# Attention scores of the second and third layer turned by the DMA crossbar instead of TensorE

## The chip, the core and the metric

The kernel runs on one core of a Trainium2 chip. A core has five engines with queues of their own: TensorE (PE in the profile; its weight loads are PEld), VectorE (DVE), ScalarE (ACT), GpSimd (POOL) and SyncE (SP), which here only issues DMA transfers. Each engine works through its queue in order and waits on semaphores for the others. The metric is the device time of one execution in microseconds; the lower, the better. A kernel's time is the median of several executions, and one more execution was taken with the profiler.

## What is computed

Input are 128 graphs of 128 nodes with 256 features each, and their adjacency matrices. Four layers follow one another; each adds its result to its input and normalizes. The first is a gated graph network of three steps, the other three are graph attention:

```python
# layer 0: three times
m = jnp.einsum('bnd,de->bne', h, weight[i])
aggr = jnp.einsum('bst,bsd->btd', A, m)
h = _gru_cell(aggr, h, w_ih, w_hh, b_ih, b_hh)
...
# layers 1 to 3
Wh = jnp.einsum('bnf,of->bno', h, W)
e = f_i[:, :, None] + f_j[:, None, :]
e = jnp.where(e > 0, e, ALPHA * e)
e = jnp.where(adj == 0, NEG_INF, e)
attention = jax.nn.softmax(e, axis=2)
h_prime = jnp.einsum('bij,bjo->bio', attention, Wh)
...
x = _layernorm(x + layer(x, adj), axis=-1)
```

Everything is float32.

## The kernel before

Four graphs make a group (G = 4), so there are 32 groups (NG). A tile of one group has 128 partitions and mostly 4x128 or 4x256 columns.

For a group, `gru` runs three steps (STEPS). A step aggregates with the adjacency matrix (L566), then makes the gates by a Strassen scheme of seven products (L508, function `strassen`): its products go to PSUM tiles of the kind "gate", which ScalarE (L574, L578, L581, L592, L605) and VectorE (L513, L615) read. Several products are added into one gate tile, so that the next product into a tile has to wait until the last value was read: `kept` copies the first product out by L574 (whole) or by L578 and L581 (in halves). Elementwise work on VectorE and GpSimd follows (L608 to L631).

Then `gat` runs three attention layers (l = 0, 1, 2). The vectors f come from VectorE (L677), are multiplied by the factor `rstd` of the layer before (L681, l > 0), turned (L689) and spread over partitions by GpSimd (L696). VectorE adds the mask (L712), ScalarE makes leaky ReLU (L716) and the exponentials with their sums (L733) into the tile `e_`. The scores must then be transposed to `pT`, because TensorE needs them with the other index on partitions (L774 multiplies by them, L785 by the layer's weights; L791 adds the residual). The normalization of a layer isn't carried out in full: its factor `rstd`, one value for each node, is multiplied onto the scores when they are transposed (l > 0). `power` computes it on GpSimd (L425).

There are two ways to transpose. Through TensorE: four transposes into a PSUM tile of the kind "bank" (L744), and an eviction which for l > 0 multiplies by `rstd` on the way (`scaled`, L749 on VectorE or four L753 on ScalarE). Through the DMA crossbar (`turned`): a copy that puts the two 16-bit halves of each number apart (L402), one crossbar transfer (L403), and a copy that puts them together again (L406). The copies appear as L299, L301 and L397 with 1024 elements of uint16. Before the change the crossbar served the turned input of groups, the GRU's state between steps, and the scores of layer l = 0; the last four groups (LAST = 4) use TensorE throughout.

The order of all instructions is made before the kernel runs, by a planner (class `Plan`). Each operation is entered with the engines it may run on and an assumed duration for each, with the tiles that it reads and writes, and with a due time. `order` plays the whole list through: an engine that is idle takes the ready operation with the earliest due time, if its buffers are free. So an engine's queue, the choice between engines, and the buffers' numbers follow from these settings:

- `LATER` gives each of a group's six stages (three GRU steps, three attention layers) a due time relative to the group's number. In the last four groups the stages go in lockstep.
- `MARGIN` is extra time in ns, after which TensorE takes an operation to be ready. `LATENCY` is that of hand-overs.
- `pools` says how many buffers of each kind there are ("gate" and "bank" share the eight PSUM banks), and `own` how many of them the oldest stage keeps for itself.
- `port`: VectorE and GpSimd share a way to memory. An operation on an engine named in its `port` starts in the plan only when no other such operation holds it. By default only GpSimd is named; most large VectorE operations on SBUF name both.

Of the kernel before, what the change touches and what calls it, by code (L numbers as in the profile page):

```python
# [13 lines left out]
ALU = mybir.AluOpType  # L14
AX = mybir.AxisListType

P = 128
D = 256
KC = D // P
G = 4  # L20
GN = G * P
H = GN // 2
STEPS = 3
# [26 lines left out]
class Plan:  # L50
# [5 lines left out]
    LATENCY = {"PE": 250, "ACT": 220, "DVE": 200, "POOL": 250, "SP": 4000}  # L56

    RUSH = 0.5
    MARGIN = 300

    def __init__(self, slots, own):
        self.free = {t: list(range(n)) for t, n in slots.items()}
# [3 lines left out]
        self.readers = {}  # L66

    def op(self, engines, fn, reads=(), writes=(), prio=0, lag=0, port=("POOL",), start=0, room=()):

        rush = self.RUSH if any((k[0] if isinstance(k, tuple) else k).tag in ("gate", "bank") for k in reads) else 0  # L70
        o = Op(engines, fn, (prio[0] - rush, len(self.ops)), lag, port)
        o.group = prio[1]
        o.earliest = start
        norm = lambda k: k if isinstance(k, tuple) else (k, 0)
        for k in map(norm, reads):
            if k in self.writer:
                o.deps.add(self.writer[k])
            self.readers.setdefault(k, []).append(o)
            o.bufs.append(k[0])
        for k in map(norm, writes):  # L80
            if k in self.writer:
                o.deps.add(self.writer[k])
            o.deps.update(self.readers.pop(k, ()))
            self.writer[k] = o
            o.bufs.append(k[0])
        o.bufs.extend(room)
        o.deps.discard(o)
        o.bufs = [b for b in dict.fromkeys(o.bufs) if b.tag]
        for b in o.bufs:
            b.left += 1  # L90
        self.ops.append(o)
# [113 lines left out]
def adj_resnorm_kernel(  # L205
# [14 lines left out]
    nc = tc.nc  # L220
    B = x.shape[0]
    NG = B // G
    LAST = 4
# [3 lines left out]
    psum = ctx.enter_context(tc.tile_pool(name="psum", bufs=1, space=bass.MemoryType.PSUM))  # L227


    pools = {"gru": 4, "xs": 2, "am": 5, "k2": 28, "k4": 18, "f": 4, "mv": 4, "st": 6, "v": 24,  # L230
             "gate": 5, "bank": 3}
    own = ({"k2": 7, "k4": 8, "gate": 1, "bank": 1, "v": 5, "st": 0}, {"k2": 5, "k4": 2, "bank": 1, "v": 5, "st": 0})
    floats = {"gru": 0, "k4": 1024, "xs": 1024, "f": 128, "mv": 8, "st": 6, "v": 4}
    tags = {t: (n, floats.get(t, 512)) for t, n in pools.items()}
    U16 = mybir.dt.uint16
    BOTH = ("DVE", "POOL")
    LATER = (-0.25, 1, -0.5, -0.5, 0, 0.25)
    plan = Plan({t: n for t, (n, _) in tags.items()}, own)
    slots = {t: [(psum if t in ("gate", "bank") else work).tile([P, w], F32, name=f"{t}{i}")
                 for i in range(n)] for t, (n, w) in tags.items() if w}  # L240
# [1 line left out]
    def T(b):  # L242
        if b.at is None:
            width = 1
            for s in b.shape:
                width *= s
            at = slots[b.tag][b.slot][:, 0:width]
            if len(b.shape) == 2:
                at = at.rearrange("p (a b) -> p a b", b=b.shape[-1])
            elif len(b.shape) == 3:  # L250
                at = at.rearrange("p (a b c) -> p a b c", b=b.shape[-2], c=b.shape[-1])
            b.at = at
        return b.at
# [133 lines left out]
    def turned(src, keys, dst, prio):  # L387


        rows = Buf("k2", GN)  # L390
        flat = lambda: T(dst) if len(dst.shape) == 1 else T(dst).rearrange("p b q -> p (b q)")
        halves_of = lambda at: at.bitcast(U16).rearrange("p (h b q) -> p h b q", h=2, b=G)
        pairs_of = lambda at: at.bitcast(U16).rearrange("p b (q h) -> p h b q", h=2)

        def together(e):
            if e == "ACT":
                nc.scalar.copy(flat().bitcast(U16).rearrange("p (q h) -> p q h", h=2),  # L397
                               T(rows).bitcast(U16).rearrange("p (h q) -> p q h", h=2))
            else:
                copy(e, flat().bitcast(U16).rearrange("p (q h) -> p h q", h=2),  # L400
                     T(rows).bitcast(U16).rearrange("p (h q) -> p h q", h=2))
        plan.op(APART, lambda e: copy(e, halves_of(flat()), pairs_of(src())), reads=keys, writes=[dst], prio=prio, port=BOTH)  # L402
        plan.op({"SP": 1200}, lambda e: nc.sync.dma_start_transpose(  # L403
            T(rows).bitcast(U16).rearrange("p (a q) -> p a q", q=P), flat().bitcast(U16)),
            reads=[dst], writes=[rows], prio=prio, lag=TURN)
        plan.op(TOGETHER, together, reads=[rows], writes=[dst], prio=prio, port=BOTH)  # L406
# [259 lines left out]
    def gat(g, xc, no, stage):  # L666


        ve, rstd = None, None
        for l in range(3):  # L670
            prio = stage(g, STEPS + l)
            if g == 0:
                score_weights(l, (prio[0], -2))
            f = Buf("f", G, P // G)
            for h in (1, 0):
# [4 lines left out]
                if l:  # L680
                    plan.op({"DVE": 100}, lambda e, h=h, f=f, rstd=rstd: nc.vector.tensor_mul(  # L681
                        T(f)[:, :, 1 - h], T(f)[:, :, 1 - h], T(rstd)), reads=[(f, 2 * b + h) for b in range(G)] + [rstd],
                        writes=[(f, 2 * b + h) for b in range(G)], prio=prio)
            e_, pT, y = Buf("k2", G, P), Buf("k2", G, P), Buf("k4", G, D)
            top, nmax, den, rden = Buf("v", G), Buf("v", G), Buf("v", G), Buf("v", G)
            b_ = bank()
            if g < NG - LAST:

                plan.op({"PE": 115}, lambda e, b_=b_, f=f: nc.tensor.transpose(  # L689
                    T(b_)[:, 0:P], T(f).rearrange("p b h -> p (b h)"), ident),  # L690
                    reads=[(f, 2 * b + 1) for b in range(G)], writes=[b_], prio=prio)
                row = Buf("k2", P)
                plan.op({"ACT": 250, "DVE": 200}, lambda e, b_=b_, row=row: copy(e, T(row), T(b_)[:, 0:P]),
                        reads=[b_], writes=[row], prio=prio)
                for b in range(G):
                    plan.op({"POOL": 300}, lambda e, row=row, b=b, e_=e_: nc.gpsimd.partition_broadcast(  # L696
                        T(e_)[:, b, :], T(row)[b * P // G:b * P // G + 1, 0:P]), reads=[row], writes=[(e_, b)], prio=prio)
                if g == NG - LAST - 1 and l == 2:

                    plan.op({"POOL": 7000}, lambda e: nc.gpsimd.load_library(library_config.standard),  # L700
                            reads=[(e_, b) for b in range(G)], writes=[Buf(None)], prio=prio)
                rows, keys, port = (lambda b, e_=e_: T(e_)[:, b, :]), lambda b: [], BOTH
            else:
                def fn(e, b_=b_, f=f):
                    for b in range(G):
                        nc.tensor.transpose(T(b_)[:, b * P:(b + 1) * P],
                                            T(f)[:, b, 0:1].to_broadcast([P, P]), ident)
                plan.op({"PE": 440}, fn, reads=[(f, 2 * b + 1) for b in range(G)], writes=[b_], prio=prio)
                rows, keys, port = (lambda b, b_=b_: T(b_)[:, b * P:(b + 1) * P]), lambda b, b_=b_: [b_], ("POOL",)
# [5 lines left out]
            for b in range(G):  # L715
                plan.op({"ACT": 285}, lambda e, b=b, f=f, e_=e_: nc.scalar.activation(  # L716
                    T(e_)[:, b, :], T(e_)[:, b, :], AF.Prelu, bias=T(f)[:, b, 1:2], alpha=SLOPE),
                    reads=[(f, 2 * b), (e_, b)], writes=[(e_, b)], prio=prio)
            if l == 1:
# [4 lines left out]
                    reads=[(top, b) for b in range(G)], writes=[some], prio=prio)  # L724
            plan.op({"DVE": 100}, lambda e, f=f, top=top: nc.vector.scalar_tensor_tensor(
                T(top), T(top), -1.0, T(f)[:, :, 1], op0=ALU.mult, op1=ALU.subtract),
                reads=[(top, b) for b in range(G)] + [(f, 2 * b) for b in range(G)],
                writes=[(top, b) for b in range(G)], prio=prio)
            plan.op({"DVE": 100}, lambda e, top=top, nmax=nmax: nc.vector.scalar_tensor_tensor(  # L729
                T(nmax), T(top), SLOPE, T(top), op0=ALU.mult, op1=ALU.min),  # L730
                reads=[(top, b) for b in range(G)], writes=[nmax], prio=prio)
            for b in range(G):
                plan.op({"ACT": 390}, lambda e, b=b, e_=e_, nmax=nmax, den=den: nc.scalar.activation(  # L733
                    T(e_)[:, b, :], T(e_)[:, b, :], AF.Exp, bias=T(nmax)[:, b:b + 1],
                    accum_out=T(den)[:, b:b + 1]), reads=[(e_, b), nmax], writes=[(e_, b), (den, b)], prio=prio)
            by_xbar = g < NG - LAST and l == 0
            if by_xbar:
                turned(lambda e_=e_: T(e_), [(e_, b) for b in range(G)], pT, prio)
            else:
                b_ = bank()  # L740

                def fn(e, b_=b_, e_=e_):
                    for b in range(G):
                        nc.tensor.transpose(T(b_)[:, b * P:(b + 1) * P], T(e_)[:, b, :], ident)  # L744
                plan.op({"PE": 440}, fn, reads=[(e_, b) for b in range(G)], writes=[b_], prio=prio)
                if l:
                    def scaled(e, b_=b_, pT=pT, rstd=rstd):
                        if e == "DVE":
                            nc.vector.tensor_mul(T(pT), T(b_).rearrange("p (b j) -> p b j", b=G),  # L749
                                                 T(rstd).unsqueeze(2).to_broadcast([P, G, P]))  # L750
                        else:
                            for b in range(G):
                                nc.scalar.mul(T(pT)[:, b, :], T(b_)[:, b * P:(b + 1) * P], T(rstd)[:, b:b + 1])  # L753
                    plan.op({"DVE": 630, "ACT": 1100}, scaled, reads=[b_, rstd], writes=[pT], prio=prio)
                else:
                    plan.op(EVICT, lambda e, b_=b_, pT=pT: copy(e, T(pT).rearrange("p b j -> p (b j)"), T(b_)),
                            reads=[b_], writes=[pT], prio=prio)
# [38 lines left out]
            rstd = power(ve, prio)  # L796
# [6 lines left out]
    def stage(g, n):  # L803

        tail = NG - LAST
        return g + LATER[n] if g < tail else tail + n, 2 * g + (n >= STEPS)

    for g in range(NG):
        gat(g, *gru(g, stage), stage)
# [50 lines left out]
```

## Time and profile before

| what | value |
|---|---|
| median of 3 executions | 2603.02 us (2602.8 to 2604.25) |
| the profiled execution | 2601.8 us, span 2600.0 us |
| granted TensorE clock | 0.998 |
| DMA moved | 117.79 MB, mean 45 GB/s |
| crossbar transfers (L403) | 200, median 3.1 us from issue to landing |
| transposes of scores on TensorE (L744) | 272 |
| their eviction with the factor | 228 L753 on ScalarE, 0.380 us each; 7 L749 on VectorE, 0.688 us each |

The span goes from the first instruction to the last. In the listings that follow, a line of a group gives the source line, the engine, the operation, written tile <- read tiles, and shapes; "x4" is the number of instructions. A line in order of time begins with its start and its duration in us, and has in brackets how long its engine was idle before it, and what ended that wait. A float32 matmul stands as two records. The durations of neighbours on one engine overlap a little, since an instruction's end is noted after the next may have begun.

### The profile page before, as it was taken

The page shows a single profiled execution, that of the slowest core. Times are in us where ns is not written, and L with a number is a line of the kernel's source. Part 1 is how long each engine was busy: PE and PEld are TensorE (multiplying, and loading weights), DVE is VectorE, ACT ScalarE, POOL GpSimd, SP SyncE. Part 2 cuts the span into 40 slices and gives each one's busy share as a digit, 9 for nine tenths or more (in the row PEclk, how much of TensorE's full clock was granted, in tenths as well). Part 3 has the DMA queues.
Part 4 walks back from the last instruction along what each step waited for, and adds up shares of the span by engine and source line. Part 5 has one row for each costly group of instructions (what it writes and reads, how often), then busy time and mean ns, then how long its engine had stood idle before and what let it go on. Part 6 is the DMA issues. An engine that isn't in the chain of part 4 may idle for free.

```text
span 2600.0 us, 41538 instructions
## 1 busy us (share of the span) xinstructions
PE 2549.3 (98%) x13484; PEld 2257.3 (87%) x13484; DVE 2124.2 (82%) x6262; ACT 1856.4 (71%) x4750; POOL 601.7 (23%) x866
## 2 busy tenths in 40 slices
PE   8999999999999999999999999999999999999988
PEld 7888888888888888888888888888888888888877
DVE  6688888978888888888888888888888887867687
ACT  5667776877778677777777776777786776665467
POOL 2022222322222221222212222212222211322011
PEclk9999999999999999999999999999999999999999
DMA  5211121312122211222121222121222121100001
GB/s 138 61 38 45 38 48 40 72 41 46 41 49 58 48 39 46 49 50 53 41 49 42 53 49 53 42 45 42 49 58 49 37 49 42 21 13 25 17 1 34
DMA packets 281307, 117.79 MB, mean 45 GB/s; under 512 B 213888, under 2 KB 279424, under 8 KB 281088
## 3 DMA queue, kind: packets, MB, share of 16 engines
q1 hardware_dynamic: 280656, 115.12, 19.1%
q8 instruction: 106, 1.74, 0.3%
q14 instruction: 113, 0.93, 0.1%
q10 hardware_dynamic: 432, 0.01, 0.0%
HBM read 45.89 MB, written 16.78 MB: 24 GB/s over the span
## 4 chain that ended last, share of the span: by engine, by line
PE 82%; DVE 10%; ACT 4%; issue 2%; DMA 1%; POOL 0%; POOLq 0%; ACTq 0%; SPq 0%; DVEq 0%
PE gate L508 59%; PE bank L785 11%; PE bank L774 6%; PE bank L566 4%; DVE k L712 2%; ACT k L733 2%; DVE nobody L677 1%; PE bank L650 1%; DVE k L513 1%; DVE k L301 1%; DVE k L791 1%; PE bank L744 1%; ACT k L299 1%; DVE v L729 1%; DVE v L722 1%
## 5 line engine op out<-in xcount | busy, mean ns | idle before, releaser
L508 PE MATMUL gate<-k,whs 128*128 128x256 f32 x4032 | 1203.3, 380 | 18.1 <-ACT k L574 15.8
L508 PE MATMUL gate<-k,wcs 128*128 128x256 f32 x4032 | 1199.3, 379 | 0.0
L508 PEld LDWEIGHTS gate<-k,wcs 128*128 128x128 f32 x4032 | 766.0, 190 | 104.2 <-issue 0.2
L508 PEld LDWEIGHTS gate<-k,whs 128*128 128x128 f32 x4032 | 736.5, 190 | 115.5 <-ACT k L574 22.5
L513 DVE TENSOR_TENSOR k<-gate,k 128x512 f32<-128x512 f32 x576 | 390.3, 684 | 145.3 <-PE gate L508 124.0
L785 PE MATMUL bank<-gwT,k 128*128 128x256 f32 x1536 | 348.7, 380 | 1.3 <-DVE k L301 1.2
L785 PEld LDWEIGHTS bank<-gwT,k 128*128 128x128 f32 x1536 | 290.5, 190 | 42.4 <-DVE k L301 2.9
L677 DVE SCALAR_TENSOR_TENSOR nobody<-k,wa 128x256 f32<-128x256 f32 x768 | 293.7, 428 | 23.1 <-ACT k L444 21.7
L425 POOL TENSOR_TENSOR v<-v,neghalf 128x4 f32<-128x4 f32 x128 | 136.0, 1062 | 731.8 <-DVE v L463 375.7
L452 ACT ACTIVATE nobody<-k 128x256 f32<-128x256 f32 x384 | 156.2, 408 | 193.2 <-DVE k L791 192.3
L299 ACT COPY k<-bank 128x512 f32<-128x512 f32 (+1 forms) x314 | 177.0, 566 | 136.9 <-PE bank L566 79.2
L397 ACT COPY k<-k 128x1024 uint16<-128x1024 uint16 x182 | 209.1, 1159 | 80.3 <-DMA k<-k 76.0
L592 ACT ACTIVATE k<-k,brz 128x256 f32<-128x256 f32 (+1 forms) x384 | 225.1, 627 | 42.4 <-DVE k L513 42.4
L791 DVE SCALAR_TENSOR_TENSOR k<-bank,v,k 128x256 f32<-128x256 f32 x384 | 167.5, 477 | 81.6 <-PE bank L785 81.3
L626 POOL TENSOR_TENSOR k<-k,k 128x512 f32<-128x512 f32 x79 | 101.3, 1282 | 506.8 <-issue 297.3
L574 ACT COPY k<-gate 128x512 f32<-128x512 f32 x288 | 166.2, 587 | 71.3 <-PE gate L508 70.7
L478 POOL TENSOR_TENSOR k<-k,k 128x256 f32<-128x256 f32 x215 | 172.2, 817 | 164.5 <-ACT k L299 69.5
L774 PEld LDWEIGHTS bank<-k,k 128*128 128x128 f32 x1536 | 188.1, 193 | 12.9 <-DVE k L791 2.1
L774 PE MATMUL bank<-k,k 128*128 128x128 f32 x1536 | 191.1, 277 | 4.8 <-DVE k L791 1.7
L733 ACT ACTIVATE k<-k,v 128x128 f32<-128x128 f32 x384 | 149.5, 397 | 47.7 <-DVE v L729 47.4
L696 POOL PARTITION_BROADCAST k<-k x336 | 114.1, 439 | 230.3 <-issue 111.2
L608 DVE SCALAR_TENSOR_TENSOR k<-k,k 128x512 f32<-128x512 f32 x192 | 148.6, 783 | 20.9 <-ACT k L605 20.3
(97 smaller groups left out, 3238.1 us busy)
## 6 DMA issues: line engine op xcount, KB each, us to landing
xs<-in_x_dram SPq DMA_DIRECT2D x32, 512.0 KB, 3.9
k<-in_x_dram SPq DMA_DIRECT2D x32, 512.0 KB, 4.1
out_dram<-k SPq DMA_DIRECT2D x32, 512.0 KB, 2.9
am<-in_adj_dram SPq DMA_DIRECT2D x32, 256.0 KB, 2.9
k<-k SPq DMA_TRANSPOSE x200, 3.1
k<-in_gnn_wT_dram SPq DMA_DIRECT2D x3, 256.0 KB, 5.0
k<-in_w_ihT_dram SPq DMA_DIRECT2D x2, 384.0 KB, 5.9
k<-in_w_hhT_dram SPq DMA_DIRECT2D x2, 384.0 KB, 6.1
```

What stands on the lines that cost most here:

```text
L299: nc.scalar.copy(dst, src)
L397: nc.scalar.copy(flat().bitcast(U16).rearrange("p (q h) -> p q h", h=2), T(rows).bitcast(U16).rearrange("p (h q) -> p q h", h=2))
L478: nc.vector if e == "DVE" else nc.gpsimd).tensor_tensor(T(t)[:, j, :], a(), b(), ALU.subtract),
L508: nc.tensor.matmul(T(dst)[:, j * H:(j + 1) * H], T(w)[:, m, gt, :], moving(m, ms)[1](), start=first and n == 0, stop=n == len(todo) - 1, s ...
L513: plan.op({"DVE": 630}, lambda e: nc.vector.tensor_add(T(o)[:, :, j * H:(j + 1) * H], T(b_).rearrange("p (g n) -> p g n", g=2), T(part).re ...
L574: plan.op({"ACT": 500}, lambda e: nc.scalar.copy(T(dst), T(src)), reads=[src], writes=[(dst, 0), (dst, 1)], prio=prio)
L592: nc.scalar.activation(T(o)[:, gt, n0:n1], src(), AF.Tanh, bias=brz[:, gt * KC + c:gt * KC + c + 1], scale=0.5)
L677: plan.op({"DVE": 345}, lambda e, b=b, h=h, l=l, f=f, xc=xc: nc.vector.scalar_tensor_tensor(next(nobody[1]), T(xc)[:, b, :], 1.0, T(wa)[:, ...
L733: plan.op({"ACT": 390}, lambda e, b=b, e_=e_, nmax=nmax, den=den: nc.scalar.activation(T(e_)[:, b, :], T(e_)[:, b, :], AF.Exp, bias=T(nmax ...
L774: nc.tensor.matmul(T(b_)[:, b * P:(b + 1) * P], T(xc)[:, b, c * P:(c + 1) * P], T(pT)[:, b, :], start=True, stop=True)
L785: nc.tensor.matmul(T(b_)[:, (b - b0) * D:(b - b0 + 1) * D], T(aT[k])[:, b * P:(b + 1) * P], T(gwT)[:, l, k, :], start=(k == 0), stop=(k == ...
L791: nc.vector.scalar_tensor_tensor(T(y)[:, b, :], T(b_)[:, (b - b0) * D:(b - b0 + 1) * D], T(rden)[:, b:b + 1], T(xc)[:, b, :], op0=ALU.mult ...
```

## The change

The transposed scores of the layers l = 1 and l = 2 go through the crossbar too, except in the last four groups. No eviction from PSUM is left there which could multiply by `rstd`; a product of its own takes its place, on GpSimd or VectorE as the planner chooses. Small column operations of VectorE (those entered with 100 ns) now name both engines as their port in the plan. The plan's settings change with it: due times, the margin, the assumed duration of L696, one more "gru" slot (a limit on the number of groups under way, without memory behind it), four "gate" and four "bank" tiles where there were five and three, and the shares in `own`. `ENDS` is empty and changes nothing.

```diff
-    MARGIN = 300
+    MARGIN = 200
...
     def op(self, engines, fn, reads=(), writes=(), prio=0, lag=0, port=("POOL",), start=0, room=()):
+        if engines == {"DVE": 100}:
+            port = ("DVE", "POOL")
...
-    pools = {"gru": 4, "xs": 2, "am": 5, "k2": 28, "k4": 18, "f": 4, "mv": 4, "st": 6, "v": 24,
-             "gate": 5, "bank": 3}
-    own = ({"k2": 7, "k4": 8, "gate": 1, "bank": 1, "v": 5, "st": 0}, {"k2": 5, "k4": 2, "bank": 1, "v": 5, "st": 0})
+    pools = {"gru": 5, "xs": 2, "am": 5, "k2": 28, "k4": 18, "f": 4, "mv": 4, "st": 6, "v": 24,
+             "gate": 4, "bank": 4}
+    own = ({"k2": 9, "k4": 8, "gate": 2, "bank": 2, "v": 5, "st": 0}, {"k2": 3, "k4": 1, "bank": 1, "v": 5, "st": 0})
...
-    LATER = (-0.25, 1, -0.5, -0.5, 0, 0.25)
+    LATER = (-0.25, 1.5, 2, 0.25, 0.5, 2)
+    ENDS = {}
...
-                    plan.op({"POOL": 300}, lambda e, row=row, b=b, e_=e_: nc.gpsimd.partition_broadcast(
+                    plan.op({"POOL": 360}, lambda e, row=row, b=b, e_=e_: nc.gpsimd.partition_broadcast(
...
-            by_xbar = g < NG - LAST and l == 0
+            by_xbar = g < NG - LAST
             if by_xbar:
                 turned(lambda e_=e_: T(e_), [(e_, b) for b in range(G)], pT, prio)
+                if l:
+                    def scaled(e, pT=pT, rstd=rstd):
+                        if e == "ACT":
+                            for b in range(G):
+                                nc.scalar.mul(T(pT)[:, b, :], T(pT)[:, b, :], T(rstd)[:, b:b + 1])
+                        else:
+                            (nc.vector if e == "DVE" else nc.gpsimd).tensor_tensor(
+                                T(pT), T(pT), T(rstd).unsqueeze(2).to_broadcast([P, G, P]), ALU.mult)
+                    plan.op({"POOL": 1300, "DVE": 620}, scaled, reads=[pT, rstd], writes=[pT], prio=prio, port=BOTH)
...
-        return g + LATER[n] if g < tail else tail + n, 2 * g + (n >= STEPS)
+        return (g + LATER[n] if g < tail else tail + n) + ENDS.get((g, n), 0), 2 * g + (n >= STEPS)
```

## The prediction

> **What bounds the kernel now.** I read the page from the top: busy shares, then the chain, then one stretch in order of time.
>
> ```profile
> PE 2549.3 (98%) x13484; PEld 2257.3 (87%) x13484; DVE 2124.2 (82%) x6262; ACT 1856.4 (71%) x4750; POOL 601.7 (23%) x866
> PE 82%; DVE 10%; ACT 4%; issue 2%; DMA 1%; POOL 0%; POOLq 0%; ACTq 0%; SPq 0%; DVEq 0%
> 900.00:1300.00 400.00, 395.77 (x2098) 351.64 (x2099) 334.74 (x988) 296.76 (x757) 93.51 (x140) 1.00 0.21 47
> ```
>
> The third line is a window in the middle of the run (columns PE, PEld, DVE, ACT, POOL, granted clock, DMA share, GB/s): TensorE is busy 99% of it at full clock, and the chain that ended last lies on it for 82% of the span. VectorE has 84% here. Busy time alone could flatter TensorE, since the ends of matmuls are modelled, so I take the step from one start to the next:
>
> ```profile
> 1002.10 0.59 PE L508 MATMUL gate<-k,wcs 128*128 128x256 f32 x2
> 1002.53 0.60 PE L744 MATMUL bank<-ident,k 128*128 128x128 f32 x4
> 1002.97 0.60 PE L508 MATMUL gate<-k,whs 128*128 128x256 f32 x2
> ...
> 1005.56 1.95 PE L774 MATMUL bank<-k,k 128*128 128x128 f32 x16
> 1007.35 0.60 PE L650 MATMUL bank<-ident,k 128*128 128x128 f32 x4
> ```
>
> A matmul of 256 columns stands as two records that take 0.43 us (1002.10 to 1002.53), 0.216 each; four transposes take 0.44 (1002.53 to 1002.97), though their bar is 0.60; sixteen 128-column records take 1.79, 0.112 each. By the page's counts: 8064+1536+24 records at 0.216 (L508, L785, L381) are 2079; 1536+1536 at 0.112 (L774, L566) 344; 740 transposes at 0.11 are 81; L353 15.5. That is 2520 us of back-to-back TensorE work in a span of 2600. The other 80 are: 5 before the first matmul, 9 after the last, some 18 of waits after 2500 us, and the rest spread out. The spread part has a clear form:
>
> ```profile
> 978.18 1.01 PE L744 MATMUL bank<-ident,k 128*128 128x128 f32 x4
> 979.18 0.58 ACT L574 COPY k<-gate 128x512 f32<-128x512 f32 x1
> 979.81 0.70 PE L508 MATMUL gate<-k,whs 128*128 128x256 f32 x2 [0.62 <-ACT k L574]
> ...
> 1058.66 0.70 PE L508 MATMUL gate<-k,whs 128*128 128x256 f32 x2 [0.62 <-ACT k L574]
> ```
>
> Once per group of four graphs (the distance is 78.85 us) TensorE waits behind a block L744 for an eviction L574, which ScalarE reaches late behind the Exp calls L733. One group's own work is 252 records L508 (54.4), 48 L785 (10.4), 48 L566 and 48 L774 (5.4 each), two L650 (0.9), three L689 (0.3), two L744 (0.9): 77.65. So 1.20 us per group is lost, and it is lost at this place.
>
> **What the Trainium skill says.** "Perfetto Trace Analysis", Identifying the Most-Contended Engine, warns that matmul busy time does not show how near TensorE is to its limit and points to the weight loads: 351.64 of 400 us (88%) agrees with a full engine. "VectorE: DVE Perf Modes", The three transpose paths, prices a 128x128 bf16 transpose at 390 ns on TensorE and 1309 ns by the crossbar, so the move lengthens latency; here four float32 blocks take 0.44 us of TensorE, and one crossbar transfer of all four lands in 3.1 us (200 of them, 3.0 to 4.8). "SBUF — State Buffer", SBUF: two separate sides, says GpSimd and VectorE take their common port as an exclusive lock for a whole instruction. The trace agrees; a 128x4 column operation ends with its neighbour on GpSimd:
>
> ```profile
> 974.71 0.90 POOL L478 TENSOR_TENSOR k<-k,k 128x256 f32<-128x256 f32 x1
> 974.95 0.68 DVE L722 TENSOR_SCALAR v<-v 128x4 f32<-128x4 f32 x1
> 976.31 0.73 POOL L478 TENSOR_TENSOR k<-k 128x256 f32<-128x256 f32 x1 [0.70 <-DVE v L725]
> 976.33 0.72 DVE L729 SCALAR_TENSOR_TENSOR v<-v 128x4 f32<-128x4 f32 x1
> ```
>
> The like-sized L761 takes 0.166.
>
> **The change, part by part.** The counts are from the order of instructions of the changed program against the old one.
>
> TensorE loses 224 transposes L744, that is 56 blocks (28 groups, two layers; the last four groups keep theirs). 56 x 0.44 = 24.6 us, and because TensorE is the full engine this is on the path. Nothing is added to it: 2495 us remain, 76.77 per group.
>
> ScalarE loses most of the scaled evictions L753 (228 to 32, 0.380 each), and the plan moves 87 PSUM copies of 0.584 from it to VectorE and gives it most of the new crossbar copies. Per group in steady flow: -8x0.380 - 4x0.584 + 4x1.042 - 1.064 + 0.27 = -2.0 us, so 58.5 falls to 56.5, 73% of a 77 us group.
>
> VectorE gets the product with the factor: 54 of 56 stand on it, two on GpSimd, whatever the two prices in the plan suggest. Priced by L631, which also reads two SBUF tiles of 128x512: 0.693. Per group 2x0.693 + 4x0.686 (PSUM copies) + 0.69 (a copy of xs) - 0.29 - 0.42 = +4.1 us: 66.0 becomes 70.1, 91% of a group. It isn't hidden by being idle time: it is hidden as long as VectorE's queue stays ahead of TensorE. Against it, the columns now keep off the port. If all of L722, L729 and L681 fell from 505, 287 and 279 to about 160 ns, a group would get 0.34+3x0.13+4x0.12 = 1.2 us back; at worst nothing, or a wait of one GpSimd operation, 0.8.
>
> The crossbar gets 256 transfers in place of 200, nine per group on SP at 1.24 us of issue each, 11 us of 77. Behind them in SP's queue stand the loads of groups ahead. DMA was busy 21%; I cost this at nothing. The bound is the latency: from Exp, copy 1.1, transfer 3.1, copy 1.16, product 0.69 and the hand-overs make some 7 us, where transpose and scaled eviction made about 2.5. In the changed order 9.5 us of TensorE work stand between the last Exp and its L774 in these layers (4.8 to 6.5 before), so some 2 us are to spare; the later due times (LATER) buy that distance. If the cover failed, each layer would lose the missing part, 0 to 2 us.
>
> Gates 5 to 4, banks 3 to 4, MARGIN 300 to 200, own: these change which hand-overs are tight. Between a gate tile's last matmul and the next one into it, the old order had at least 1.73 us of TensorE work in steady flow. The new order has 0.97 once per group (two L508 of another gate and one L689), with L578 and L581 (0.478+0.374) to be done in it. TensorE's end lies 0.16 behind its step (379 against 216 ns) and the two hand-overs cost 0.04 and 0.05 in the stretch shown, so 1.10 is needed: 0.13 short, with the slow restart about 0.25 if ScalarE is free, up to 1.2 if it is as late as it was before. I take 0.6. The old stall of 1.20 sat beside a block that is gone. Over 24 steady groups the new one is 14 us; the old kernel lost 19x1.2 there and 5.7 in six single waits between 440 and 600 us, 28.5 together: -14. Bounds: -22 and 0.
>
> Head and tail: after the last L508 73.9 us of TensorE work remain in the new order, 71.6 before; the last four groups keep due times and transposes, and the last 100 us I leave as they are, within 6 either way. For new waits that I can't place (VectorE at 91%) I add 6, bounds 0 and 30.
>
> Sum: -24.6 - 14 + 6 = -33 on the profiled 2601.8 us (span 2600.0). The median shown is 1.2 above that: 2603 - 33 = 2570.
>
> **The rivals.**
> *Only the transposes count (0.25).* The waits stay as large in sum as they were: 2603 - 24.6 = 2578, between 2574 and 2592. For it: any order fitted this tightly has some late hand-over. Against: its one periodic stall is gone.
> *VectorE takes the bound in the steady part (0.18): slower.* At 91% in a fixed order, a late eviction of a gate (L513, 0.684; hand-overs with 1.73 us of TensorE work and this reader rise from 22 to 72) stalls TensorE several times per group. Break-even: 24.6 over 26 groups is 0.95, so from 2.15 us lost per group in place of 1.20 it is slower. At 3.2 it costs 26x2.0 = 52, less 24.6: 2630. Against it: at 84% VectorE made TensorE wait almost nowhere (L513 1.7 us in all, L791 1.7).
> *The freed time is eaten (0.07).* About 2.15 us per group: 2598 to 2608.
> *The layers' longer way isn't covered.* 56 layers short by 0.5 us would be 28: it falls under the last two.
>
> **How the numbers follow.** The forecast (2556 to 2585, 2570 likeliest) has 0.50. Faster by over 0.2% (5 us, what a measurement of this kernel can tell from no change) is 0.50+0.25 = 0.75; same 0.07; slower 0.18. The range goes from 2556, the good bounds of the steady waits, to 2606, which leaves out the slower case and a little below.
>
> **What would show it.** TensorE's busy time near 2525; 48 records of L744 left; the distance between like matmuls of neighbouring groups 77 to 77.6 us, where 78.85 was; no wait of L508 on L574 once per group, but a short one on L581; VectorE near 2220 busy, ScalarE near 1815; L722 and L729 below 0.2 us. A distance above 79 us, with L508, L774 or L785 waiting on VectorE, makes the prediction wrong; so does a last stretch over 110 us.

## The result and the profile after

The changed kernel takes 2610.93 us (2605.12 to 2612.24, 11 runs) against 2603.02 (2601.81 to 2604.25, 11 runs): a ratio of 1.0027, 95% interval 1.0019 to 1.0036. It is slower by 8 us, where 2570 was forecast. The span of the profiled execution is 2609.6 us. Lines from 71 on are two or three higher than before, those behind the new product twelve: L508 is L511, L677 is L680, L689 is L692, L681 is L684, L626 is L629, L744 is L756, L774 is L786, L785 is L797; the new product is L748.

The page of the changed kernel, busy times and chain:

```profile
PE 2531.2 (97%) x13260; PEld 2228.8 (85%) x13260; DVE 2208.7 (85%) x6393; ACT 1850.5 (71%) x4555; POOL 661.4 (25%) x895
...
PE 76%; DVE 13%; DMA 6%; ACT 3%; issue 2%; POOL 0%; SPq 0%; POOLq 0%; ACTq 0%; DVEq 0%
```

TensorE's busy time fell by 18 us and its 224 transposes are gone, but the chain lies on TensorE for 76% of the span and no longer for 82%: it waits more. The window in the middle of the run (PE, PEld, DVE, ACT, POOL, clock, DMA share, GB/s) says the same, since TensorE has 390 of 400 us where it had 396:

```profile
900.00:1300.00 400.00, 390.34 (x2052) 344.75 (x2051) 351.50 (x1008) 292.92 (x717) 103.99 (x145) 1.00 0.25 53
```

What TensorE waits for, longest in total first (us in total, times, longest):

```profile
PE bank L692 <- DVE nobody L680: 26.9, 26, 1.1
PE bank L692 <- DVE f L684: 7.4, 16, 0.5
PE bank L653 <- DVE k L634: 7.1, 4, 4.0
PE gate L511 <- ACT k L584: 6.4, 10, 1.4
```

In the kernel before, lines of the same view were these:

```profile
PE gate L508 <- ACT k L574: 15.8, 21, 2.5
...
PE bank L689 <- DVE nobody L677: 2.6, 5, 0.9
PE bank L689 <- DVE f L681: 2.3, 3, 1.1
```

The old wait on the eviction of a gate (L508 on L574) has shrunk from 15.8 us to 1.6 (L511 on L577). In its place stands L692, the transpose of the score vectors: one small matmul, 26 times late by about 1.1 us for the sums L680, and 16 times by about 0.5 for L684, their product with the factor. The first of the regular waits on L680 and the last, TensorE alone:

```profile
233.15 0.33 PE L692 MATMUL bank<-ident,f 128*128 128x128 f32 x1 [1.05 <-DVE nobody L680]
...
2135.89 0.33 PE L692 MATMUL bank<-ident,f 128*128 128x128 f32 x1 [1.05 <-DVE nobody L680]
```

There is one such wait in each of the groups between, and these two lie 24 groups apart: 79.28 us per group. Of these 76.77 are work (the prediction's count), so 2.51 are lost, where it was 1.20. The prediction's own break-even of 2.15 is passed: 26 groups x (2.51 - 1.20) = 34, less 24.6, is +9.5 us; measured +7.9.

### The profile page after: what moved, and what is told of

It is laid out like the page before. It is cut to its first block, busy times and chain, and to the rows that moved or that the text cites. A ratio compares the mean times of both kernels' runs of the same rounds, so it can differ in the third digit from the quotient of the medians.

```text
span 2609.6 us, 41097 instructions
## 1 busy us (share of the span) xinstructions
PE 2531.2 (97%) x13260; PEld 2228.8 (85%) x13260; DVE 2208.7 (85%) x6393; ACT 1850.5 (71%) x4555; POOL 661.4 (25%) x895
## 4 chain that ended last, share of the span: by engine, by line
PE 76%; DVE 13%; DMA 6%; ACT 3%; issue 2%; POOL 0%; SPq 0%; POOLq 0%; ACTq 0%; DVEq 0%
PE gate L511 58%; PE bank L797 6%; PE bank L786 5%; DVE nobody L680 5%; DMA k<-k 5%; PE bank L569 4%; DVE k L304 2%; DVE k L803 1%; PE bank L653 1%; DVE k L516 1%; DVE k L611 1%; DMA xs<-in_x_dram 1%; DVE k L615 1%; PE bank L692 1%; ACT k L400 1%
## 5 line engine op out<-in xcount | busy, mean ns | idle before, releaser
L511 PE MATMUL gate<-k,whs 128*128 128x256 f32 x4032 | 1207.8, 381 | 9.7 <-ACT k L584 6.4
L511 PE MATMUL gate<-k,wcs 128*128 128x256 f32 x4032 | 1200.7, 379 | 1.4 <-ACT wcs L302 1.4
L511 PEld LDWEIGHTS gate<-k,wcs 128*128 128x128 f32 x4032 | 766.9, 190 | 106.5 <-ACT wcs L302 1.8
L511 PEld LDWEIGHTS gate<-k,whs 128*128 128x128 f32 x4032 | 739.8, 191 | 112.6 <-ACT k L584 10.3
L516 DVE TENSOR_TENSOR k<-gate,k 128x512 f32<-128x512 f32 x576 | 390.0, 685 | 125.9 <-PE gate L511 106.8
L428 POOL TENSOR_TENSOR v<-v,neghalf 128x4 f32<-128x4 f32 x128 | 145.7, 1138 | 1138.1 <-DVE v L466 614.6
L797 PE MATMUL bank<-gwT,k 128*128 128x256 f32 x1536 | 351.4, 380 | 5.7 <-ACT k L302 4.3
L797 PEld LDWEIGHTS bank<-gwT,k 128*128 128x128 f32 x1536 | 289.6, 190 | 50.5 <-ACT k L302 8.6
L680 DVE SCALAR_TENSOR_TENSOR nobody<-k,wa 128x256 f32<-128x256 f32 x768 | 315.2, 455 | 11.6 <-PE bank L692 10.5
L400 ACT COPY k<-k 128x1024 uint16<-128x1024 uint16 x194 | 225.9, 1165 | 109.3 <-DMA k<-k 99.9
L577 ACT COPY k<-gate 128x512 f32<-128x512 f32 x288 | 165.6, 576 | 125.3 <-PE gate L511 123.1
L595 ACT ACTIVATE k<-k,brz 128x512 f32<-128x512 f32 (+1 forms) x384 | 227.7, 627 | 32.6 <-DVE k L516 31.7
L629 POOL TENSOR_TENSOR k<-k,k 128x512 f32<-128x512 f32 x94 | 124.0, 1320 | 419.6 <-ACT k L624 396.9
L481 POOL TENSOR_TENSOR k<-k,k 128x256 f32<-128x256 f32 x205 | 170.8, 846 | 153.1 <-DVE k L634 65.0
L786 PEld LDWEIGHTS bank<-k,k 128*128 128x128 f32 x1536 | 186.9, 193 | 9.3 <-DVE k L748 2.7
L719 ACT ACTIVATE k<-k,f 128x128 f32<-128x128 f32 x384 | 128.6, 395 | 89.6 <-DVE v L715 89.1
L786 PE MATMUL bank<-k,k 128*128 128x128 f32 x1536 | 189.0, 276 | 2.3 <-DVE k L748 1.0
L302 ACT COPY k<-bank 128x512 f32<-128x512 f32 (+2 forms) x240 | 128.6, 538 | 79.7 <-PE bank L786 28.4
L304 DVE COPY k<-bank 128x512 f32<-128x512 f32 (+1 forms) x264 | 156.2, 600 | 32.2 <-PE bank L786 15.8
L624 ACT ACTIVATE k<-k,bi 128x512 f32<-128x512 f32 x192 | 138.1, 720 | 49.9 <-DVE k L621 37.9
```

Source lines behind the costliest of these rows:

```text
L304: nc.vector.tensor_copy(dst, src)
L481: nc.vector if e == "DVE" else nc.gpsimd).tensor_tensor(T(t)[:, j, :], a(), b(), ALU.subtract),
L511: nc.tensor.matmul(T(dst)[:, j * H:(j + 1) * H], T(w)[:, m, gt, :], moving(m, ms)[1](), start=first and n == 0, stop=n == len(todo) - 1, s ...
L516: plan.op({"DVE": 630}, lambda e: nc.vector.tensor_add(T(o)[:, :, j * H:(j + 1) * H], T(b_).rearrange("p (g n) -> p g n", g=2), T(part).re ...
L577: plan.op({"ACT": 500}, lambda e: nc.scalar.copy(T(dst), T(src)), reads=[src], writes=[(dst, 0), (dst, 1)], prio=prio)
L595: nc.scalar.activation(T(o)[:, gt, n0:n1], src(), AF.Tanh, bias=brz[:, gt * KC + c:gt * KC + c + 1], scale=0.5)
```

## Where the new wait comes from

One such place in full, changed kernel, in order of time:

```profile
942.53 0.42 DVE L680 SCALAR_TENSOR_TENSOR nobody<-k,wa 128x256 f32<-128x256 f32 x1
...
942.87 0.42 DVE L680 SCALAR_TENSOR_TENSOR nobody<-k,wa 128x256 f32<-128x256 f32 x1
...
942.99 1.42 POOL L629 TENSOR_TENSOR k<-k,k 128x512 f32<-128x512 f32 x1 [3.63 <-ACT k L624]
...
943.11 0.59 PE L511 MATMUL gate<-k,wcs 128*128 128x256 f32 x2
...
943.22 1.48 DVE L680 SCALAR_TENSOR_TENSOR nobody<-k,wa 128x256 f32<-128x256 f32 x1
...
944.62 0.08 DVE L680 DVE_READ_ACCUMULATOR nobody<-k,wa 128x1 f32 x1
...
944.76 0.33 PE L692 MATMUL bank<-ident,f 128*128 128x128 f32 x1 [1.05 <-DVE nobody L680]
...
945.12 0.42 DVE L680 SCALAR_TENSOR_TENSOR nobody<-k,wa 128x256 f32<-128x256 f32 x1 [0.42 <-PE bank L692]
```

A layer has eight L680, each a sum into one column of `f`: four for h = 1, then four for h = 0. Only the first four are needed for what is made from L692. The sum that begins at 943.22 is the sixth. It should take 0.42 us and takes 1.48, because L629 on GpSimd, which began 0.23 us earlier, holds the common port until 944.41. TensorE stands ready at 943.55 and starts when the sixth sum is there, and the seventh sum then waits for L692 in turn.

Both waits, that of L692 for the fifth and sixth sum and that of the seventh sum for L692, are false: no value asks for them. The plan enters L692 as a reader of (f, 2b+1), the four it uses; but it turns the whole tile `f`, so the program that is built must also wait for any sum of the other kind that stands ahead of it in the order. In the old order 82 of the 84 transposes of this kind stood behind all eight sums, far enough that it mattered little (L689 waited 4.9 us in all). In the new order 25 of 84 stand behind six.

The second wait of L692, 16 times, stands behind the port too, with GpSimd's subtraction L481 ahead of the multiplication of the four sums by the factor. But this product is one that L692 needs:

```profile
1049.61 1.01 POOL L428 TENSOR_TENSOR v<-v,neghalf 128x4 f32<-128x4 f32 x1 [9.60 <-DVE v L459]
...
1050.59 0.73 POOL L481 TENSOR_TENSOR k<-k 128x256 f32<-128x256 f32 x1
...
1050.65 0.76 DVE L684 TENSOR_TENSOR f<-f,v 128x4 f32<-128x4 f32 x2
...
1051.47 0.33 PE L692 MATMUL bank<-ident,f 128*128 128x128 f32 x1 [0.45 <-DVE f L684]
```

Two 128x4 products take 0.76 us: they begin as GpSimd hands over the factor, 0.06 us after its next operation has taken the port. Of the two, only the product of the four unneeded sums, the short one at the end, is waited for without need.

So theory F was: the wait of 1.05 us is a false one, for sums that stand behind the port. The rival, theory V, was the prediction's slower case: VectorE with 88% of its time taken is late in general, so that a wait taken away at one place comes back at the next.

## Experiments on the same order

These change what an instruction waits for or how long it holds the port, and leave the order on every engine as it was; only *The factor on GpSimd* moves one product, and *The transposes put back* adds four. Their edits are shown shortened.

**Columns of their own.** The four sums that L692 does not use move to columns 112 to 115 of `f`, and L692 turns columns 0 to 111. What reads the four sums follows them (not shown):

```diff
-    accum_out=T(f)[:, b, 1 - h:2 - h]
+    accum_out=T(f)[:, b, 0:1] if h else side(f)[:, b:b + 1]     # side: columns 112 to 115
...
-    T(b_)[:, 0:P], T(f).rearrange("p b h -> p (b h)"), ident
+    T(b_)[0:112, 0:P], T(f).rearrange("p b h -> p (b h)")[:, 0:112], ident
```

> The changed kernel in the same order on every engine; only the four sums that the score transpose L692 does not need get columns of their own (112 to 115 of f), and L692 turns columns 0 to 111. So L692 waits for the fourth sum L680 (or the first L684) and no longer for the sixth (or the second). Theory F (a false wait): in about 25 groups the wait of 1.21 us of L692 on L680 goes, and the wait of 0.62 on L684 shrinks by some 0.1; 25 x 1.21 = 30, so about 2580 (2574 to 2590). Theory V (VectorE at 88% is late in general): the wait moves to the next reader of VectorE's work and the time stays at 2604 or more.

Measured: 2579.46 us (2577.36 to 2581.18), ratio to the kernel before 0.9911 (0.9896 to 0.9926). That is 31.5 us less than the changed kernel, and faster than both. Its trace shows the same sums at the same place (lines are four higher: L684 for L680, L696 for L692, L633 for L629):

```profile
933.89 1.42 POOL L633 TENSOR_TENSOR k<-k,k 128x512 f32<-128x512 f32 x1 [3.64 <-ACT k L628]
...
934.12 1.48 DVE L684 SCALAR_TENSOR_TENSOR nobody<-k,wa 128x256 f32<-128x256 f32 x1
...
934.45 0.27 PE L696 MATMUL bank<-ident,f 128*112 128x128 f32 x1
...
934.55 0.60 PE L515 MATMUL gate<-k,whs 128*128 128x256 f32 x2
```

The sixth sum is held as long as before, 1.48 us, and TensorE passes it. The window 900 to 1300 us of this kernel:

```profile
900.00:1300.00 400.00, 395.46 (x2085) 350.83 (x2084) 352.88 (x1019) 295.78 (x720) 105.12 (x145) 1.00 0.26 54
```

VectorE is as busy as in the changed kernel (352.88 against 351.50), and TensorE is at 99% again. The wait did not come back elsewhere, so for this order theory V falls. Two things stay. One is the second wait of L692, here L696:

```profile
PE bank L696 <- DVE f L688: 7.0, 19, 0.4
```

It was 7.4 us in the changed kernel, so it was a needed wait for the most part. The other is the loss per group: the same transpose stands at 233.21 and, 24 groups later, at 2107.12, which is 78.08 us per group, and 1.31 lost. That is no less than the 1.20 of the kernel before.

**The same columns in the kernel before.**

> The kernel before with the same columns of their own. There only some of the score transposes stand between the eight sums, and none of its regular waits is on L677. Both theories: no change, 2600 to 2604. If it falls by 10 us or more, the edit itself is worth something that theory F does not explain.

Measured: 2599.8 us, ratio 0.9987 (0.9979 to 0.9996): 3 us, just under the range that both theories gave, and a tenth of what it brings to the changed order. In this trace the five waits of L689 on L677, 2.6 us together, are gone, so the 3 us are about what the same false wait cost in the old order. The edit brings little beyond that.

**The port given up halfway.** L629 on GpSimd is issued as two halves of 256 columns.

```diff
-    nc.gpsimd.tensor_tensor(T(d), T(h_), T(v)[:, 0, :], ALU.subtract)
+    for n in (0, H):
+        nc.gpsimd.tensor_tensor(T(d)[:, n:n + H], T(h_)[:, n:n + H], T(v)[:, 0, n:n + H], ALU.subtract)
```

> The changed kernel in the same order, with the GpSimd subtraction L629 (128x512, 1.3 us) issued as two of 256 columns, so that the common port is given up in the middle. Theory F with the lock: the sixth L680 is held for a half only, the wait of 1.21 us on L692 falls to about 0.6, 25 x 0.6 = 15: about 2596 (2588 to 2602). If the lock has no part in it, L680 is as late as before and the time stays at 2608 to 2612. Theory V: no gain either.

Measured: 2597.51 us (2594.37 to 2601.67), ratio 0.9982 (0.9976 to 0.9989), 13.4 less than the changed kernel. Its trace, same place (L681 for L680, L693 for L692):

```profile
940.67 1.75 POOL L629 TENSOR_TENSOR k<-k,k 128x256 f32<-128x256 f32 x2 [3.64 <-ACT k L624]
...
940.89 0.94 DVE L681 SCALAR_TENSOR_TENSOR nobody<-k,wa 128x256 f32<-128x256 f32 x1
...
941.90 0.33 PE L693 MATMUL bank<-ident,f 128*128 128x128 f32 x1 [0.51 <-DVE nobody L681]
```

The sixth sum is held for 0.94 and not 1.48 us, and TensorE's wait falls from 1.05 to 0.51. Over the whole run the waits for these sums fall from 26.9 to 13.5 us, by as much as the gain. So the lock sets the length of the false wait. Halves and columns of their own together:

> The changed kernel with columns of their own (2579) and L629 on GpSimd in two halves. With the false wait gone nothing that TensorE waits for stands behind L629: no gain, 2576 to 2581. A gain like that of the halves alone (13 us) would say that the lock costs in other places too.

Measured: 2580.5 us (2578.22 to 2581.57), as with the columns alone. Where TensorE does not wait behind it, the lock costs nothing.

**The factor on GpSimd.** On top of the columns of their own, the four sums are multiplied on GpSimd right behind the operation that makes the factor.

```diff
     order = plan.order()
+    for f, rstd, o in early:                 # L684 for h = 1
+        order.remove(o)
+        o.engine = "POOL"
+        order.insert(1 + max(order.index(d) for d in o.deps if d in order), o)
```

> The changed kernel with columns of their own (2579) and the same order, except that the four sums which L692 needs are multiplied by the factor on GpSimd, directly behind the operation that makes the factor, and not on VectorE (L684), which is held by the GpSimd subtraction that follows. Theory F says that this hold makes the wait of 0.5 us on L692 once per group: it goes. What the prediction priced in the same place, the gate handed over by L581 and L584 with 0.97 us of TensorE work between, is then bare: at 0.25 us per group the gain is 24 x 0.25 = 6 (2573), at 0.5 it is nothing (2579), and at nothing it is 12 (2567).

Measured: 2577.93 us (2574.93 to 2579.88), ratio 0.9902 (0.9888 to 0.9917); its interval overlaps that of the columns alone (0.9896 to 0.9926), so no gain is shown. TensorE in order of time (L701 is the transpose, L515 the gates):

```profile
1039.86 0.59 PE L515 MATMUL gate<-k,wcs 128*128 128x256 f32 x2
1040.41 0.32 PE L701 MATMUL bank<-ident,f 128*112 128x128 f32 x1
1040.79 0.70 PE L515 MATMUL gate<-k,whs 128*128 128x256 f32 x2
1041.33 0.59 PE L515 MATMUL gate<-k,wcs 128*128 128x256 f32 x2
```

The transpose is now 0.12 us late (1040.41 for 1039.86 + 0.43), but the next gate product starts 0.38 after it where a transpose takes 0.11, and takes 0.10 longer itself: 0.49 us in sum. The last two, 0.37, are the hand-over of the gate (L578 and L581 in the prediction, L581 and L584 in the changed kernel, L585 and L588 here): in the trace this product starts as L588 ends. In the changed kernel it lies hidden beneath the wait of L692, which is just ahead of it, so removing the one wait uncovers the other.

**The transposes put back.** The kernel with columns of their own gets four transposes of `pT` in front of L786 in the two layers, into the bank tile that L786 overwrites.

```diff
     def fn(e, b_=b_, c=c, pT=pT, xc=xc):
+        if by_xbar and l and not c:
+            for b in range(G):
+                nc.tensor.transpose(T(b_)[:, b * P:(b + 1) * P], T(pT)[:, b, :], ident)
```

> The changed kernel with columns of their own (2579) and the same order, with four transposes of pT put in front of L786 in the second and third layer of 28 groups; what they write is overwritten by L786. So TensorE gets the 56 x 0.44 = 24.6 us back that the change took from it, and nothing else changes. If TensorE's work counts in full on the path, as the prediction took it: 2604 (2600 to 2606). If waits take the room anyway: 2580 to 2595.

Measured: 2605.01 us (2603.07 to 2606.89), 25.5 more than without, where 24.6 were counted. TensorE's work counts on the path at its full price.

## Experiments on the settings

Here the planner makes another order each time.

**Old scores with the new settings, and new scores with the old settings.** The first undoes the crossbar path alone (`by_xbar = g < NG - LAST and l == 0`); the second keeps it and puts `LATER`, `MARGIN`, `pools` and `own` back (the column rule and the assumed duration of L696 stay new).

> The changed kernel's settings (due times, margin, gates and banks, shares, column port), but the scores of the second and third layer turned by TensorE with the scaled eviction as before. TensorE's work is 24.6 us more than in the changed kernel. In its order 23 score transposes L692 (of the 84 and the 48 of the last groups) stand behind six of the eight sums. Theory F: the false wait is made by the order that these settings give, so it appears here too: 2603 + 20 to 30 = 2622 to 2635. Theory V (the load that the crossbar path puts on VectorE): with the old load the waits are those of the kernel before, 2596 to 2610.

> The crossbar for the scores of all three layers, the product with the factor and the column port, but due times, margin, gates and banks, gru slots and shares as in the kernel before. The order is another one: 29 score transposes stand between their eight sums, in differing places. Theory F: the wait comes from where the order of the new settings puts L692 and L629, so with the old settings it is smaller, and the 24.6 us of TensorE work show: 2580 to 2595. Theory V: VectorE carries the same new work, so the time is 2604 to 2620. The old due times leave the longer way from Exp to L786 less cover; if that bites, waits of L786 on L400 or L748 show and the time is above 2610 with them.

Measured: 2669.98 us (ratio 1.0256, 1.0239 to 1.0274) and 2658.53 (ratio 1.0212, 1.0197 to 1.0227). The first lies above every range given, the second above all but the open one of its last sentence.

| | scores by TensorE | scores by the crossbar |
|---|---|---|
| old settings | 2603.0 | 2658.5 |
| new settings | 2670.0 | 2610.9 |

So the change is not the sum of its parts: each part alone costs 55 to 67 us, both together 8. Which waits cost it differs. With the settings alone TensorE waits for gate evictions on VectorE (first fence), with the crossbar and the old settings for few but long ones (second fence; us in total, times, longest):

```profile
PE gate L511 <- DVE k L516: 41.0, 26, 1.9
PE bank L692 <- DVE f L684: 12.7, 12, 1.8
```

The false wait is there too, but smaller than theory F said (L692 on L680, 8.7 us in 13 waits), so it explains little of this run.

```profile
PE bank L569 <- DVE k L304: 20.5, 3, 8.0
PE gate L511 <- ACT k L577: 17.8, 7, 5.4
PE bank L692 <- DVE nobody L680: 11.2, 8, 6.1
PE bank L653 <- DVE k L634: 9.3, 3, 6.7
PE bank L786 <- DVE k L748: 8.7, 6, 4.1
```

L786 on L748 is the longer way from Exp that the old due times cover less well; it is a part of the second case, not the whole. Another part is the clock: it is 0.991 and 0.983 in these two runs and 0.998 in the kernel before. One minus the clock, times the span, is 24 and 45 us against 5; this is an upper estimate of what the lower clock cost, since TensorE was idle in some of that time. The last section shows such a place.

**The margin, and the column rule.** `MARGIN` back to 300; the two lines on `port` in `op` taken out; and the margin with columns of their own.

> The changed kernel with the planner's margin for TensorE at 300 ns as before, all else as changed; it is planned anew. 22 score transposes stand between the seventh or fifth and the eighth sum, three behind the sixth, where 25 stood behind the sixth. Theory F: the wait depends on where L629 falls; with a margin of 0.1 us more a wait of 1.21 shrinks by no more than 0.1 where the place is the same, and goes where it is another: 2580 to 2606. If the smaller margin were the cause by itself (a tight plan in general), all of the short waits go: 2575 to 2585. Theory V: 2604 or more.

> The changed kernel without the column rule: in the plan the small column operations of VectorE no longer keep off the common port. Planned anew, so the order moves. If the rule is worth what its reading promises, L725, L732 and L684 get longer again (mean above 0.2 us) and the time rises by up to 10 us on what the order gives else. Theory F: decided by the wait of L692 on L680 in this order: 2580 to 2606 when it is gone, 2606 to 2620 when it stays.

> Margin 300 and the columns of their own together. Theory F: no false wait is left, and a wait of 0.5 us per group on L684 shrinks by the margin: 2568 to 2580, as fast as the changed order with columns of their own (2579) or faster. Theory V: no faster than 2600.

Measured: 2659.38 us (ratio 1.0219, 1.0204 to 1.0234), 2645.2 (1.0161, 1.0145 to 1.0176) and 2641.77 (1.0147, 1.013 to 1.0164). All three lie above every range with an upper end by 25 us or more; only theory V's open ones (2604 or more, no faster than 2600) hold the first and the third. Without the column rule the false wait is nearly gone (the transpose, here L690, waits 2.8 us for the sums), and the kernel is slower all the same, by hand-overs of gates (here L509 is the gate product, L575 and L514 its readers):

```profile
PE gate L509 <- ACT k L575: 26.8, 48, 1.6
PE gate L509 <- DVE k L514: 20.1, 28, 2.2
```

In the margin's order the columns of their own bring 17.6 us, less than the 31.5 of the changed order. What these runs show is that either of these two settings, moved by itself, costs 34 us (the column rule) and 48 us (the margin; 62 with the columns), through an order with other late hand-overs. Some of these fit theory V: with the margin at 300, TensorE waits 22.2 us for gates that VectorE reads late (L511 on L516). But VectorE's load doesn't explain it. It is busy for 2198.6 us there and for 2201.6 in the faster kernel with columns of their own; and with the settings alone, where these waits are the largest (41.0 us), it is busy for only 2140.3. Why the plan's order comes out tight at other places for each of them was not followed further; that stays open.

## Why the prediction was wrong

These steps were right. TensorE is the full engine and 24.6 us of its work go: put back, they cost 25.5. The periodic wait of L508 on L574 goes. The loads came near what was counted: VectorE 2208.7 us busy (forecast 2220), TensorE 2531 (2525), 48 records L756; ScalarE 1850 was 35 above its forecast. The gate hand-over with 0.97 us between was put at 0.6 us per group; bare, at the place shown, it is 0.37. The small column operations got shorter: L722 of 505 ns on average is L725 of 174, L729 of 287 is L732 of 154; L681 stays long (279, now 258), and at the place shown it follows the factor at once and meets L481. Not all of this is the column rule's work: in the run without it L725 is back at 523, but L732 is at 168 and L684 at 214. The transfers stayed at 3.1 us, and no regular wait of L786 on the longer way shows.

The step that failed is the term for steady waits. Its larger miss is the last part: "For new waits that I can't place (VectorE at 91%) I add 6, bounds 0 and 30." The two waits of L692 are those new waits, 1.21 us in each group and 0.62 in 16 of 25 from start to start, and they are most of the 2.51 us per group. Taking the false part of them away gave 31.5 us, more than the upper bound alone. The kernel then took 2579 and not 2570, because the other part failed as well: the steady waits were to fall by 14, and without the false wait 1.31 us per group are still lost, where 1.20 were before and 0.6 was counted. What is left in that trace before the last groups is above all the transpose waiting for the product with the factor (7.0 us), gate products waiting for a copy on ScalarE (L515 on L588, 6.7) and L801 for another (L306, 4.2). That is what *Only the transposes count* said (2578): the waits stay as large in sum as they were. The false wait could have been placed before the run: the order of instructions shows the score transpose behind six of eight sums, the code shows that it reads the whole tile, and the lock was quoted in the prediction itself. I had looked at hand-overs of gates and banks alone, and taken the plan's list of what an operation reads for what the program waits for.

The slower rival had the right direction, and the 2.51 us lost per group lie between its break-even of 2.15 and its own 3.2; but it had the wrong cause. Not VectorE's load, and not L513, but one 0.42 us sum that GpSimd holds up for 1.06 and that TensorE waits for without need.

## What to carry to other kernels

Where a planner orders the work, its list of reads and writes must be that of the program: an operation that touches a whole tile waits for every earlier write into it, used or not. Give values that go to different readers columns or tiles of their own. And before pricing a change that makes everything tighter, look in the new order for each small instruction on the full engine and count what stands ahead of it, a lock on another engine included.

## What the runs showed that was not expected

A wait of TensorE can cost more than its length. In the kernel with the crossbar and the old settings, one of 5.37 us is followed by this:

```profile
1125.74 0.59 PE L511 MATMUL gate<-k,whs 128*128 128x256 f32 x2
...
1132.13 1.22 PE L511 MATMUL gate<-k,whs 128*128 128x256 f32 x2 [5.37 <-ACT k L577]
1133.14 1.06 PE L511 MATMUL gate<-k,wcs 128*128 128x256 f32 x2
1134.00 1.06 PE L511 MATMUL gate<-k,whs 128*128 128x256 f32 x2
...
1138.14 0.60 PE L511 MATMUL gate<-k,whs 128*128 128x256 f32 x2
```

From 1132.13 to 1138.14 a pair of 256-column records takes 0.86 us or more where it takes 0.43 otherwise, so another 3 us go; the granted clock between 1130 and 1135 is 0.53. The Trainium skill, "TensorE: Matmul & The Clock Gate", Why this matters for your kernels, warns of idle gaps over some 3 us, after which the clock is back at half. This wait agrees. But shorter waits can do it too, as in the run with the settings alone:

```profile
508.24 0.70 PE L511 MATMUL gate<-k,whs 128*128 128x256 f32 x2 [1.91 <-DVE k L516]
...
509.33 1.06 PE L511 MATMUL gate<-k,whs 128*128 128x256 f32 x2
510.18 1.06 PE L511 MATMUL gate<-k,wcs 128*128 128x256 f32 x2
```

In that run TensorE has 14 waits of 1.8 to 1.9 us, and the clock is at half for 3.4 us after nine of them. After the 25 regular waits of 1.05 us in the changed kernel it never is: there the product behind L692 starts 0.16 us after it where 0.11 is usual, and no more is lost. What decides in between, the runs don't show.
